# A layer's own products added by VectorE straight out of PSUM, and another order of work between the edge sort and layer 0

## Chip, cores and metric

The kernel runs on one core of a Trainium2 chip. The metric is the device time of one execution in microseconds (us). Times below come from three timed runs and from one profiled execution, whose trace gives the start and length of each instruction on the five engines: PE (matmul), DVE (VectorE), ACT (ScalarE), POOL (GpSimd) and SP (which only issues transfers here).

## The reference, cut to what matters

Two layers act on X, 6250 nodes with 256 features, over 100,000 weighted edges. In layer 0 the normalised rows go through two matrices: `x @ weight_l` gives the messages, which are gathered by source, weighted and summed by row, and `x @ weight_r` is the node's own product, added to the node itself with both biases:

```python
def _L0_gnn_ref(x, edge_row, edge_col, edge_val, weight_l, bias_l, weight_r, bias_r):
    h = x @ weight_l
    msgs = edge_val[:, None] * h[edge_col]
    agg = jax.ops.segment_sum(msgs, edge_row, num_segments=N)
    out = agg + bias_l
    out = out + x @ weight_r + bias_r
    return out
...
x = x + _L0_gnn_ref(_layernorm(x, axis=-1), src, dst, edge_weight, ...)
x = x + _L0_ffn_ref(_layernorm(x, axis=-1)[None], ...)[0]
x = x + _L1_gnn_ref(_layernorm(x, axis=-1), src, dst, edge_weight, ...)
x = x + _L1_ffn_ref(_layernorm(x, axis=-1)[None], ...)[0]
```

The feed-forward part of layer 0 has 8 experts of two hidden layers each, all of them computed and weighted by a softmax gate. Layer 1 sums messages by destination, and then computes 32 experts, of which each row keeps one.

## The kernel before, in words

X stays on the chip as 49 tiles of 128 rows. The work has three stages.

**The sort, 0 to about 391 us.** The edges have to be arranged by the tile of their row. They come in 25 groups (`for g in range(NG)`), and each group passes through four helpers. `count_group` makes one-hots of the tile of each edge (`hot` L454, `four`, `mine`) on VectorE and counts them by matmuls (L464 to L474); ACT evicts the counts as `start` (L472) and `total` (L476). `settle_group` keeps the running counts (`ZJ` L482, `wrap` L484, `base_of` L486, `full_of` L488). `place_group` works out each edge's place (`same` L497, `picked` L506, `pos` L516, `over` L519, `place_b` L521), makes the one-hot `to` (L523) from it, and multiplies the payload in five pieces into `loads` (four on VectorE, L527; one in 32 scaled activations on ACT, L502). PE's 32 `put` matmuls (L530) then throw the payload to its places; ACT evicts it as `there` (L533), and POOL adds it into Z (L535 to L539).

Layer 0's dense products ride along in the same loop, two tiles a group. `center0` takes bn_stats of X (L547) and centres X on ACT (`xn`, L556). `products0` transposes xn on PE, evicts the transpose on ACT (`nT`, L341), multiplies it with both matrices at once into one PSUM tile `ph` (L570; two halves of 256 columns, messages and own products), evicts all of `ph` on ACT, scaled by rstd (`hs`, L571), and POOL adds the second half and the bias to X (L572, L573). The first half is written to DRAM as h0 on SP's queue.

**Layer 0, to about 1830 us.** `edges0` reads a block's edges out of ZJ and Z into idx, w and dl (VectorE, L671 to L686). For each tile 18 indirect gathers are issued on POOL (L201); ACT and VectorE make m, the weighted row in two parts (L230, L231), VectorE makes one-hots s (L222), and PE sums into `acc` (L701), which VectorE adds to X (L704). These column steps form a stream (`aggregate0`), which a plan (`aheads`, `upto`) interleaves with the experts of the block before: `begin0` (norm, transposes, gates), `hidden0` (matmuls L748, eviction hT on ACT, L751), `outs0` (py L760, addition to X on VectorE, L762) and `end0` (h1, norm for layer 1). Blocks have 1, 1, 2, 3, then nine times 4, and 3 and 3 tiles. `missing` prepares what layer 1's early columns lack.

**Layer 1, to the end.** Gathers of h1 by sorted columns, then the 32 experts (`hidden1`, `outs1`, L984 to L1000), and the output.

The code gives the order in which a scheduler meets the instructions; the scheduler sets the order on each engine by its own priorities, and `tc.issue_after(ins)` pins an instruction behind another. Engines issue in order. Layer 0's weights (`w1`, `w2`, `wo`: 2 MB each) are loaded on ACT's queue when the sort's memory comes free, behind which `bo` and `gT` are cleared on VectorE (L641, L644).

Of the kernel before, what the change touches and what calls it, by code (L numbers as in the profile page):

```python
# [16 lines left out]
P = 128  # L17
N = 6250
D = 256
# [30 lines left out]
def gnn_ffn_kernel(ctx: ExitStack, tc: tile.TileContext, a, out):  # L50
# [59 lines left out]
    dl_c = const.tile([P, NCOL], F32, name="dl_c")  # L110
# [79 lines left out]
    bias0 = across("L0_gnn_bias_l", early)  # L190
    bias0r = across("L0_gnn_bias_r", early)
    nc.gpsimd.tensor_add(bias0, bias0, bias0r)
# [33 lines left out]
    def weighted(pool, h, idx, w, ahead, parts):  # L226

        g = gather(pool, h, idx, ahead)
        m = pool.tile([P, 2, D], F32R, tag="m", name="m", bufs=parts)
        nc.scalar.activation(m[:, 0, :], g, AF.Copy, scale=w)  # L230
        nc.vector.scalar_tensor_tensor(m[:, 1, :], g, w, m[:, 0, :], op0=OP.mult, op1=OP.subtract)  # L231
        return m

    halves = {}

# [101 lines left out]
    def transposed(psum, xn, to):  # L337
        tr = psum.tile([P, 2, P], F32, tag="tr", name="tr", bufs=1)
        for k in range(2):
            nc.tensor.transpose(tr[:, k, :], xn[:, k * P:(k + 1) * P], ident)  # L340
        nc.scalar.activation(to, tr, AF.Copy)  # L341

    def norm(psum, t, mean, rstd, to):

        xn = work.tile([P, D], F32, tag="xn", name="xn")
        nc.vector.tensor_scalar(xn, X[:, t, :], mean, rstd, op0=OP.subtract, op1=OP.mult)
        transposed(psum, xn, to)
# [99 lines left out]

    def count_group(g):
# [42 lines left out]
    def place_group(g, hot, start):  # L491
# [9 lines left out]
        for c in range(GC):  # L501
            nc.scalar.activation(loads[:, NPAY - 1, c // 4, :, c % 4], hot[:, c // 4, :, c % 4], AF.Copy,  # L502
                                 scale=last[:, g * GC + c:g * GC + c + 1])
# [9 lines left out]
        with nc.allow_low_precision(reason="counts below 256"):  # L513
            for h in range(2):
# [8 lines left out]
        nc.vector.tensor_tensor(to, place_b[:, :, None, :].to_broadcast([P, CB, P, 4]),  # L523
                                which_q[:, None, :, :].to_broadcast([P, CB, P, 4]), OP.is_equal)
# [10 lines left out]
        nc.gpsimd.tensor_add(there[:, 0], there[:, 0], there[:, 1])  # L535
        nc.gpsimd.tensor_scalar(some[:, 0], there[:, 0], 0.0, from_p[:, g:g + 1], op0=OP.is_gt, op1=OP.mult)
        nc.gpsimd.tensor_add(Z[:, 0, :, g], there[:, 0], some[:, 0])
        nc.gpsimd.tensor_add(some[:, 1], there[:, 2], there[:, 3])
        nc.gpsimd.tensor_add(Z[:, 1, :, g], some[:, 1], there[:, 4])  # L539

    def center0(tiles):

        n = len(tiles)
        mv = work.tile([P, NB, 2], F32, tag="mv", name="mv")
        for j, t in enumerate(tiles):
            st = work.tile([P, 6], F32, tag="st", name="st", bufs=4)
            nc.vector.bn_stats(st, X[:, t, :])  # L547
            nc.vector.bn_aggr(mv[:, j, :], st)
        std = work.tile([P, NB], F32, tag="std", name="std", bufs=3)
        nc.vector.tensor_scalar(std[:, :n], mv[:, :n, 1], LN_EPS, None, op0=OP.add)  # L550
        shift = work.tile([P, NB], F32, tag="shift", name="shift")
        nc.vector.tensor_scalar(shift[:, :n], mv[:, :n, 0], -1.0, None, op0=OP.mult)
        nc.scalar.activation(std[:, :n], std[:, :n], AF.Sqrt)
        xn = early.tile([P, 2, D], F32, tag="xn0", name="xn0", bufs=2)
        for j, t in enumerate(tiles):
            nc.scalar.activation(xn[:, j, :], X[:, t, :], AF.Identity, bias=shift[:, j:j + 1])  # L556
        return tiles, xn, std

    def products0(tiles, xn, std):
# [4 lines left out]
        hs = early.tile([P, 2, 2, D], F32, tag="hs", name="hs", bufs=2)  # L564
        for j, t in enumerate(tiles):
# [5 lines left out]
            nc.scalar.activation(hs[:, j], ph, AF.Copy, scale=rstd[:, j:j + 1])  # L571
            nc.gpsimd.tensor_add(X[:, t, :], X[:, t, :], hs[:, j, 1, :])  # L572
            nc.gpsimd.tensor_add(X[:, t, :], X[:, t, :], bias0)  # L573
        nc.sync.dma_start(h0[tiles[0] * P:(tiles[0] + n) * P, :].rearrange("(t p) d -> p t d", p=P), hs[:, :n, 0, :])
# [4 lines left out]
    centered = center0(pairs[0])  # L579
    settle_group(0, *counted[2:])  # L580
    for g in range(NG):
        now, tiles0 = counted, centered
        if g + 1 < NG:
            counted = count_group(g + 1)
        products0(*tiles0)
        place_group(g, *now[:2])
        if g + 1 < NG:
            centered = center0(pairs[g + 1])
            settle_group(g + 1, *counted[2:])
        if g == 1:  # L590
            check_edges()
            prep_ctx.close()
# [3 lines left out]
    nc.vector.tensor_reduce(most[:, 0:1], sizes.rearrange("p t g -> p (t g)"), AX.X, OP.max)  # L596
    tot = early.tile([P, NT], F32, name="tot")
    nc.vector.scalar_tensor_tensor(tot, full_of[0], float(P), base_of[0], op0=OP.mult, op1=OP.add)
    nc.vector.tensor_reduce(most[:, 1:2], tot, AX.X, OP.max)
    nc.vector.tensor_scalar(most[:, 0:1], most[:, 0:1], float(P), None, op0=OP.is_gt)  # L600
    nc.vector.tensor_scalar(most[:, 1:2], most[:, 1:2], float(P * EW), None, op0=OP.is_gt)
    nc.vector.tensor_max(bads[0], bads[0], most[:, 0:1])
    nc.vector.tensor_max(bads[0], bads[0], most[:, 1:2])
    nc.vector.tensor_copy(badis[0], bads[0])
    nc.vector.tensor_scalar(good, bads[0], 1.0, None, op0=OP.is_lt)
    nc.vector.tensor_max(bads[1], bads[1], bads[0])
    nc.vector.tensor_copy(badis[1], bads[1])
    nc.vector.tensor_scalar(good1, bads[1], 1.0, None, op0=OP.is_lt)
    nc.vector.tensor_scalar(off, bads[1], float(DST_PAD), None, op0=OP.mult)
    nc.vector.tensor_scalar(dl_c, dl_c, off, None, op0=OP.add)  # L610
# [24 lines left out]
    with tc.tile_pool(name="layer0", bufs=1) as wp, tc.tile_pool(name="outs0", bufs=1, side="right") as wo_pool, \  # L635
            tc.tile_pool(name="psum_y0", bufs=1, space=bass.MemoryType.PSUM) as psum_y:
        wr = wp.tile([P, 2, NX0], F32, name="wr")
        nc.scalar.dma_start(wr, a["L0_ffn_Wr"].rearrange("(k p) e -> p k e", p=P))

        bo = wp.tile([P, D], F32, name="bo")  # L640
        nc.vector.memset(bo, 0.0)  # L641
        nc.scalar.dma_start(bo[:NX0, :], a["L0_ffn_bo"])
        gT = wp.tile([P, NB * P], F32, name="gT")
        nc.vector.memset(gT, 0.0)  # L644
        bn = wp.tile([P, 2, 5, 2 * NX0], F32, name="bn")
        nc.scalar.dma_start(bn, a["bn"])
        wo = wo_pool.tile([P, NX0, 2, D], F32, name="wo")
        for w, name in ((w1, "L0_ffn_W1"), (w2, "L0_ffn_W2"), (wo, "L0_ffn_Wo")):
            nc.scalar.dma_start(w.rearrange("p e k h -> p (e k) h"), a[name].rearrange("e (k p) h -> p (e k) h", p=P))


        scale = wp.tile([P, 2, 2 * NX0], F32, name="scale")
        shift = wp.tile([P, 2, 2 * NX0], F32, name="shift")
        nc.vector.tensor_scalar(scale, bn[:, :, 4, :], BN_EPS, None, op0=OP.add)
        nc.scalar.activation(scale, scale, AF.Sqrt)
        nc.vector.reciprocal(scale, scale)
        nc.vector.tensor_mul(scale, scale, bn[:, :, 1, :])  # L657
        nc.vector.tensor_sub(shift, bn[:, :, 0, :], bn[:, :, 3, :])
        nc.vector.tensor_mul(shift, shift, scale)
        nc.vector.tensor_add(shift, shift, bn[:, :, 2, :])  # L660

        def edges0(tiles):
# [23 lines left out]
            nc.vector.tensor_copy(dl[:, :n], bothi[:, :n])  # L686
# [3 lines left out]
        edges = [edges0(blocks0[0]), edges0(blocks0[1])]  # L690

        def aggregate0():
            for b, tiles in enumerate(blocks0):
                idx, dl, w = edges[b]
                for i, t in enumerate(tiles):
                    acc = psum.tile([P, 2, D], F32, tag="agg", name="acc", bufs=2)
                    for j in range(EW):
# [3 lines left out]
                        nc.tensor.matmul(acc, s[:, j % SJ, :], m, start=(j == 0), stop=(j == EW - 1))  # L701
                        if j == EW - 1:
# [9 lines left out]
        def begin0(tiles):  # L712
# [5 lines left out]
            for j in range(n):  # L718
                for k in range(2):
                    nc.tensor.matmul(pl[:, j, :], nT[:, k, j * P:(j + 1) * P], wr[:, k, :],  # L720
                                     start=(k == 0), stop=(k == 1))
# [33 lines left out]
        def outs0(block, e, hT):  # L755
            tiles, _, gate = block
            for j, t in enumerate(tiles):
                py = psum_y.tile([P, D], F32, tag="y", name="py", bufs=2)
                for k in range(2):
                    nc.tensor.matmul(py, hT[:, k, j * P:(j + 1) * P], wo[:, e, k, :],  # L760
                                     start=(k == 0), stop=(k == 1))
                nc.vector.scalar_tensor_tensor(X[:, t, :], py, gate[:, j, e:e + 1], X[:, t, :],  # L762
                                               op0=OP.mult, op1=OP.add)
# [124 lines left out]
        plans[-1] = [cum[-1] + (NE - tail + CS // 2 + 3) * max(0, u + 1 - head) / (2 * NX0 - head) for u in range(2 * NX0)]  # L888
        sums.upto(cum[0])
        block = begin0(blocks0[0])  # L890
        first = hidden0(0, block, 0, block[1])
        for b in range(nblk):
            final = b + 1 == nblk
            for e in range(NX0):
                if e == 0 and b + 2 < nblk:
# [3 lines left out]
                if b == nblk - 3 and e == 3:  # L899
                    small1()  # L900
                    early_columns()
                if final and e == 5:
                    fill = missing()
                if final and e >= 5:
                    next(fill)
                sums.upto(plans[b][2 * e])
# [8 lines left out]
                sums.upto(plans[b][2 * e + 1])  # L915
# [194 lines left out]
```

## Time and profile before

| what | us |
|---|---|
| timed runs, median (lowest to highest) | 2901.26 (2896.87 to 2902.55) |
| profiled execution, its own time | 2895.13 |
| span of its trace | 2893.4 |
| mean granted TensorE clock (share of full speed) | 0.974 |
| busy: PE / DVE / ACT / POOL | 2677.7 / 2012.4 / 1626.1 / 1926.1 |
| from one `to` to the next in the sort (151.59 to 165.89) | 14.30 |
| last `to` of the sort starts | 379.28 |
| first gather of layer 0 | 397.79 |
| first `acc` matmul of layer 0 | 413.75 |

The profile cuts the span into 40 slices of 72 us, and gives each engine's busy tenths:

```profile
PE   5888848888999999999999998779999999999998
DVE  8999977778768767766566555666666666666630
PEclk9999978999999999999999999999999999999999
DMA  4000043333333333333332214333333333333310
```

A digit 9 is 90% or more; PEclk is the clock that TensorE was granted, in tenths. The first five slices are the sort, the sixth holds the crossing into layer 0, the 26th and its neighbours the crossing into layer 1. Timeline rows have the start, the length, the engine, the line, the operation with output and inputs, and in brackets the idle time before it with what ended it. Group rows have the count, then busy us and mean ns of one instruction, then idle before them and what released it.

### The profile page before, as it was taken

What the parts mean: (1) busy time and instruction counts of PE and PEld (TensorE: products, weight loads), DVE (VectorE), ACT (ScalarE), POOL (GpSimd) and SP (SyncE); (2) the same over time, 40 slices, a digit from 0 to 9 for tenths busy, and PEclk for the clock granted to TensorE, in tenths of its full rate; (3) what the DMA queues carried; (4) which work ended last, traced back from release to release, by engine and by line L of the source; (5) the groups of instructions that cost most, each with busy time, mean ns of one, the idle gap of its engine ahead of it and who ended that gap; (6) DMA issues with size and microseconds to landing.
All of it is one profiled execution on the core that took longest, in us unless ns stands there. A gap on an engine that the chain in (4) does not pass through costs nothing.

```text
span 2893.4 us, 37030 instructions
## 1 busy us (share of the span) xinstructions
PE 2677.7 (93%) x10336; PEld 1750.2 (60%) x10336; DVE 2012.4 (70%) x4917; ACT 1626.1 (56%) x3790; POOL 1926.1 (67%) x1932
## 2 busy tenths in 40 slices
PE   5888848888999999999999998779999999999998
PEld 2444427665566666666666665556666666666666
DVE  8999977778768767766566555666666666666630
ACT  6777737655555555555555545455555555555532
POOL 4666667777767676766675527677777777777720
PEclk9999978999999999999999999999999999999999
DMA  4000043333333333333332214333333333333310
GB/s 150 19 19 19 19 141 97 101 100 102 92 99 95 90 101 97 91 100 96 91 102 82 78 39 135 109 108 103 107 108 109 106 108 102 108 106 109 109 44 12
DMA packets 123140, 260.73 MB, mean 90 GB/s; under 512 B 32236, under 2 KB 68904, under 8 KB 122920
## 3 DMA queue, kind: packets, MB, share of 16 engines
q0 software_dynamic: 79872, 218.21, 26.2%
q1 hardware_dynamic: 31672, 32.42, 3.4%
q10 hardware_dynamic: 11376, 7.60, 0.8%
q8 instruction: 85, 1.39, 0.2%
q14 instruction: 135, 1.11, 0.1%
HBM read 238.87 MB, written 19.25 MB: 89 GB/s over the span
## 4 chain that ended last, share of the span: by engine, by line
PE 65%; DVE 17%; DMA 8%; issue 4%; ACT 4%; POOL 1%; ACTq 0%; POOLq 0%; DVEq 0%
PE ph L748 19%; PE py L760 10%; PE py L1000 9%; PE ph L984 9%; PE acc L701 6%; PE acc L277 4%; DMA g<-h,src_c 4%; DMA g<-h,idx 3%; DVE loads L527 3%; DVE to L523 2%; DVE m L231 2%; ACT m L230 2%; PE ph L987 1%; PE ph L214 1%; POOL g L201 1%
## 5 line engine op out<-in xcount | busy, mean ns | idle before, releaser
L201 POOL DMA_INDIRECT g<-h,idx x882 | 903.1, 1024 | 391.8 <-DVE m L231 175.2
L201 POOL DMA_INDIRECT g<-h,src_c x718 | 725.6, 1011 | 227.8 <-issue 104.2
L230 ACT ACTIVATE m<-g,w 128x256 fp32r<-128x256 f32 x882 | 394.7, 500 | 260.0 <-PE acc L701 136.0
L751 ACT ACTIVATE hT<-ph,shift,scale 128x512 f32<-128x512 f32 (+3 forms) x480 | 329.0, 696 | 314.6 <-PE ph L748 313.4
L230 ACT ACTIVATE m<-g,val_c 128x256 fp32r<-128x256 f32 x718 | 349.7, 503 | 273.6 <-PE acc L277 132.2
L231 DVE SCALAR_TENSOR_TENSOR m<-g,val_c,m 128x256 fp32r<-128x256 f32 x718 | 337.1, 483 | 211.2 <-ACT m L230 207.6
L231 DVE SCALAR_TENSOR_TENSOR m<-g,w,m 128x256 fp32r<-128x256 f32 x882 | 397.7, 476 | 42.5 <-ACT m L230 41.4
L748 PE MATMUL ph<-nT,w 128*128 128x512 f32 (+3 forms) x960 | 373.1, 524 | 25.0 <-ACT hT L751 24.8
L760 PE MATMUL py<-wo,hT 128*128 128x256 f32 x1568 | 382.1, 387 | 13.8 <-DVE X L762 10.5
L1000 PE MATMUL py<-w,hm 128*128 128x256 f32 x1568 | 386.7, 385 | 3.1 <-ACT hm L989 3.1
L701 PE MATMUL acc<-m,s 128*128 128x512 f32 x882 | 341.4, 490 | 38.0 <-DVE scale L657 24.7
L984 PE MATMUL ph<-nT,w 128*128 128x512 f32 (+2 forms) x832 | 374.8, 571 | 0.0
L748 PE MATMUL ph<-hT,w 128*128 128x512 f32 (+3 forms) x960 | 368.5, 518 | 0.5 <-ACT hT L751 0.5
L760 PEld LDWEIGHTS py<-wo,hT 128*128 128x128 f32 x1568 | 294.7, 193 | 80.8 <-DVE X L762 26.9
L277 PE MATMUL acc<-m,s 128*128 128x512 f32 x782 | 332.2, 499 | 1.7 <-DVE m L231 1.7
L1000 PEld LDWEIGHTS py<-w,hm 128*128 128x128 f32 x1568 | 292.1, 193 | 52.9 <-ACT hm L989 4.6
L222 DVE TENSOR_TENSOR s<-col,dl 128x384 fp32r<-128x384 f32 x294 | 161.4, 551 | 187.0 <-PE acc L701 184.8
L748 PEld LDWEIGHTS ph<-nT,w 128*128 128x128 f32 x960 | 175.2, 195 | 174.2 <-issue 118.1
L989 ACT ACTIVATE hm<-ph,b 128x512 f32<-128x512 f32 (+2 forms) x208 | 136.8, 659 | 200.0 <-PE ph L987 199.6
L748 PEld LDWEIGHTS ph<-hT,w 128*128 128x128 f32 x960 | 176.2, 193 | 118.9 <-issue 88.3
L701 PEld LDWEIGHTS acc<-m,s 128*128 128x128 f32 x882 | 169.7, 195 | 109.8 <-issue 48.9
L984 PEld LDWEIGHTS ph<-nT,w 128*128 128x128 f32 x832 | 157.2, 191 | 101.5 <-issue 81.1
(248 smaller groups left out, 3359.0 us busy)
## 6 DMA issues: line engine op xcount, KB each, us to landing
g<-h,idx POOLq DMA_INDIRECT x882, 2.8
g<-h,src_c POOLq DMA_INDIRECT x718, 2.8
h<-hs SPq DMA_DIRECT2D x25, 256.0 KB, 2.1
X<-in_x_dram SPq DMA_DIRECT2D x12, 512.0 KB, 8.9
out_dram<-o SPq DMA_DIRECT2D x11, 512.0 KB, 3.4
h<-hs SPq DMA_DIRECT2D x9, 512.0 KB, 3.0
w<-in_L_ffn_W_dram ACTq DMA_DIRECT2D x2, 2048.0 KB, 11.2
wo<-in_L_ffn_Wo_dram ACTq DMA_DIRECT2D x1, 2048.0 KB, 20.0
```

What stands on the lines that cost most here:

```text
L201: nc.gpsimd.indirect_dma_start(out=g, out_offset=None, in_=h, in_offset=bass.IndirectOffsetOnAxis(ap=idx, axis=0))
L222: nc.vector.tensor_tensor(s[:, :n], col[:, None, :].to_broadcast([P, n, P]), dl[:, j:j + n, None].to_broadcast([P, n, P]), OP.is_equal)
L230: nc.scalar.activation(m[:, 0, :], g, AF.Copy, scale=w)
L231: nc.vector.scalar_tensor_tensor(m[:, 1, :], g, w, m[:, 0, :], op0=OP.mult, op1=OP.subtract)
L277: nc.tensor.matmul(acc, s[:, (j - js.start) % SJ, :], m, start=opens, stop=done)
L701: nc.tensor.matmul(acc, s[:, j % SJ, :], m, start=(j == 0), stop=(j == EW - 1))
L748: nc.tensor.matmul(ph[:, :nw], (w1, w2)[layer][:, e, k, m * P:(m + 1) * P], src[:, k, :nw], start=(k == 0), stop=(k == 1))
L751: nc.scalar.activation(hT[:, m, :nw], ph[:, :nw], AF.Relu, bias=shift[:, layer, c:c + 1], scale=scale[:, layer, c:c + 1])
L760: nc.tensor.matmul(py, hT[:, k, j * P:(j + 1) * P], wo[:, e, k, :], start=(k == 0), stop=(k == 1))
L984: nc.tensor.matmul(ph[:, :nw], w1f[:, k, c * P:(c + 1) * P], nT[:, k, :nw], start=(k == 0), stop=False)
L989: nc.scalar.activation(hm[:, :nw], ph[:, :nw], AF.Relu, bias=b1[:, c:c + 1])
L1000: nc.tensor.matmul(py[:, j, :], now[:, cols], w2f[:, c, :], start=False, stop=(c == NC1 - 1), skip_group_check=True)
```

## The change

Layer 0's own products: ACT evicts only the messages' half of `ph`, 128x256 instead of 128x512. VectorE adds the other half to X in one scalar_tensor_tensor straight from PSUM (X = ph * rstd + X). POOL's two additions a tile are gone. The bias goes elsewhere: POOL splits the sum of both biases into three bf16 pieces at the start (rows 0, 32 and 64 of `bias0_b`), and each tile's `acc` in layer 0 gets one more bf16 matmul with `ones_b`. The second half of ACT's 32 scaled pieces is issued behind the pair's last eviction. The statistics of a pair are taken one group earlier (`stats0`).

The order between sort and layer 0: the last group's `to` is made in two halves, the checks stand behind it, and the last additions into Z go to VectorE. The first block's edges come first; the weights are loaded behind them on SP's queue, then the second block's edges. `wo`, whose memory is free early, is loaded in the sort: in the built order it stands on SP's queue right behind the second h0 write. The third block's edges come in the middle of the first block's columns. The columns that are issued beside the first two experts of the first block stand behind its norm, transposes and gates. `small1`, `early_columns` and `missing` stand behind the newest addition of `outs0`. `dl_c` becomes bf16. The blocks stay as they were.

The diff, cut to its core:

```diff
     def place_group(g, hot, start, evicted):
...
         for c in range(GC):
-            nc.scalar.activation(loads[:, NPAY - 1, c // 4, :, c % 4], hot[:, c // 4, :, c % 4], AF.Copy,
-                                 scale=last[:, g * GC + c:g * GC + c + 1])
+            with ExitStack() as behind:
+                for ins in evicted[-1:] if c >= GC // 2 else ():
+                    behind.enter_context(tc.issue_after(ins.ins))
+                nc.scalar.activation(loads[:, NPAY - 1, c // 4, :, c % 4], hot[:, c // 4, :, c % 4], AF.Copy,
+                                     scale=last[:, g * GC + c:g * GC + c + 1])
...
-        nc.vector.tensor_tensor(to, place_b[:, :, None, :].to_broadcast([P, CB, P, 4]),
-                                which_q[:, None, :, :].to_broadcast([P, CB, P, 4]), OP.is_equal)
+        final = g == NG - 1
+        step = CB // 2 if final else CB
+        for b in range(0, CB, step):
+            bs = slice(b, b + step)
+            placed = nc.vector.tensor_tensor(to[:, bs], place_b[:, bs, None, :].to_broadcast([P, step, P, 4]),
+                                             which_q[:, None, :, :].to_broadcast([P, step, P, 4]), OP.is_equal)
...
-            nc.scalar.activation(hs[:, j], ph, AF.Copy, scale=rstd[:, j:j + 1])
-            nc.gpsimd.tensor_add(X[:, t, :], X[:, t, :], hs[:, j, 1, :])
-            nc.gpsimd.tensor_add(X[:, t, :], X[:, t, :], bias0)
+            evicted.append(nc.scalar.activation(hs[:, j], ph[:, 0, :], AF.Copy, scale=rstd[:, j:j + 1]))
+            nc.vector.scalar_tensor_tensor(X[:, t, :], ph[:, 1, :], rstd[:, j:j + 1], X[:, t, :],
+                                           op0=OP.mult, op1=OP.add)
...
-        products0(*tiles0)
-        place_group(g, *now[:2])
+        evicted = products0(*tiles0)
+        placed, there, some = place_group(g, *now[:2], evicted)
         if g + 1 < NG:
-            centered = center0(pairs[g + 1])
+            end_group(g, there, some, nc.gpsimd)
+        if g + 1 < NG:
+            centered = center0(*measured)
+            if g + 2 < NG:
+                measured = stats0(pairs[g + 2])
             settle_group(g + 1, *counted[2:])
...
+    with tc.issue_after(told.ins):
+        end_group(NG - 1, there, some, nc.vector)
...
-        edges = [edges0(blocks0[0]), edges0(blocks0[1])]
+        told = []
+        edges = [edges0(blocks0[0])]
+        behind = ExitStack()
+        behind.enter_context(tc.issue_after(told[0].ins))
...
+        for w, name in ((w1, "L0_ffn_W1"), (w2, "L0_ffn_W2"), (wo, "L0_ffn_Wo")):
+            nc.sync.dma_start(w.rearrange("p e k h -> p (e k) h"), a[name].rearrange("e (k p) h -> p (e k) h", p=P))
...
+        edges.append(edges0(blocks0[1]))
+        behind.close()
...
                         nc.tensor.matmul(acc, s[:, j % SJ, :], m, start=(j == 0), stop=(j == EW - 1))
+                        if j == 0:
+                            nc.tensor.matmul(acc[:, 0, :], ones_b, bias0_b, start=False, stop=False,
+                                             skip_group_check=True)
...
+        sums.upto(cum[0] // 2)
+        with tc.issue_after(newest["rest"].ins):
+            edges.append(edges0(blocks0[2]))
         sums.upto(cum[0])
         block = begin0(blocks0[0])
+        normed = [newest[k] for k in ("xn", "nT", "gates")]
...
                 if b == nblk - 3 and e == 3:
-                    small1()
-                    early_columns()
+                    with tc.issue_after(newest["out"].ins):
+                        small1()
+                        early_columns()
```

In the changed code the eviction is line 604, the addition from PSUM line 605, `to` line 546 and the bias matmul line 752.

## Prediction

> **What bounds the kernel now.** I read the busy shares by stage first, because the change touches one stage and the crossing behind it. In these rows of the table of windows, the columns are window, its length, then PE, PEld, DVE, ACT and POOL busy (instructions), granted clock, DMA share, GB/s.
>
> ```profile
> 100.00:150.00 50.00, 43.60 (x201) 22.71 (x199) 50.00 (x109) 38.72 (x144) 29.91 (x35) 1.00 0.05 17
> 250.00:300.00 50.00, 43.65 (x188) 21.80 (x187) 50.00 (x109) 41.32 (x153) 34.42 (x38) 1.00 0.07 22
> 380.00:400.00 20.00, 7.40 (x32) 3.80 (x32) 12.60 (x47) 0.38 (x1) 6.34 (x9) 0.72 0.37 119
> 400.00:420.00 20.00, 6.24 (x13) 3.64 (x13) 19.45 (x54) 6.43 (x14) 15.92 (x14) 0.51 0.89 306
> ```
>
> In the sort VectorE is never idle; PE has 13% to spare. From 380 to 420 us PE is mostly idle: the crossing. So I went to VectorE's and POOL's timelines for one group of the sort. From one `to` (L523) to the next is 165.89 - 151.59 = 14.30 us; from the third group's `to` (80.1) to the last (379.28) 21 periods average 14.25.
>
> ```profile
> 151.59 2.27 DVE L523 TENSOR_TENSOR to<-place_b,which_q 128x4096 bf16<-128x4096 bf16 x1
> 153.94 0.76 DVE L482 SCALAR_TENSOR_TENSOR ZJ<-base_of,part,full_of 128x49 bf16<-128x49 bf16 x1
> 154.58 0.73 DVE L484 TENSOR_SCALAR wrap<-total 128x49 f32<-128x49 f32 x1
> 155.42 0.67 DVE L486 TENSOR_TENSOR base_of<-total,wrap 128x49 bf16<-128x49 f32 x1
> 156.97 0.88 DVE L497 TENSOR_TENSOR same<-tq 128x256 bf16<-128x256 bf16 x1
> ```
>
> ```profile
> 151.85 2.60 POOL L572 TENSOR_TENSOR X<-X,hs 128x256 f32<-128x256 f32 x1 [0.56 <-ACT hs L571]
> 154.53 0.74 POOL L573 TENSOR_TENSOR X<-X,L_gnn_bias_l_b 128x256 f32<-128x256 f32 x1
> 155.23 0.79 POOL L572 TENSOR_TENSOR X<-X,hs 128x256 f32<-128x256 f32 x1
> 156.09 1.47 POOL L573 TENSOR_TENSOR X<-X,L_gnn_bias_l_b 128x256 f32<-128x256 f32 x1
> ```
>
> The four VectorE operations lie beside POOL's four additions and take 0.76 + 0.73 + 0.67 + 0.88 = 3.04 us. Where POOL adds nothing, at 19 to 37 us, the same four took 0.41, 0.19, 0.20 and 0.40: 1.20. So the additions cost VectorE about 1.84 us a group, and its own work is 14.29 - 1.84 = 12.45.
>
> Then I read PE's and ACT's timelines of the same group, because the new operation waits for both.
>
> ```profile
> 153.92 7.38 PE L530 MATMUL put<-loads,to 128*128 128x245 bf16 x32
> 163.26 1.99 PE L570 MATMUL ph<-wlr,nT 128*128 128x512 f32 x4
> ```
>
> ```profile
> 162.84 0.37 ACT L341 ACTIVATE nT<-tr 128x256 f32<-128x256 f32 x1
> 165.33 0.69 ACT L571 ACTIVATE hs<-ph,rstd 128x512 f32<-128x512 f32 x1
> ```
>
> The reader is to see an order on PE: `put` (7.20 us until the count matmuls at 161.12), count, and only then the products `ph`. Nothing that leads to the next `to` depends on `ph` today.
>
> **The change in the sort.** Removed: POOL's four additions a pair (-1.84 us of VectorE's time). Added on VectorE: two scalar_tensor_tensor of 128x256 out of PSUM. The nearest row, which reads PSUM and X in the same form, is the layer's own addition:
>
> ```profile
> L762 DVE SCALAR_TENSOR_TENSOR X<-py,gate,X 128x256 f32<-128x256 f32 x392 | 186.7, 479 | 36.4 <-PE py L760 34.4
> L998 PE MATMUL py<-b,hotT 128*128 128x256 bf16 x49 | 13.4, 273 | 0.0
> ```
>
> Its 479 ns include overlap; start to start such additions follow each other at 0.39. VectorE's own work becomes 12.45 + 0.78 = 13.23 us. By work alone the sort would gain 1.06 us a group.
>
> But the additions are placed ahead of `to`. The built order of the changed kernel shows two kinds of group in turn. In kind A the first addition (L605) stands behind the loads and ahead of over, rstd, two bn_stats, place_b and `to`; the second stands behind `to`. In kind B both stand ahead of `to`, with two `loads` and pos between them. Each addition waits in that order for ACT's eviction of the other half of the same PSUM tile. `to` is what PE's next `put` waits for, and the `ph` that the addition reads stands on PE behind the previous `put`. So a loop closes that was open before. From the start of a `to`:
> - to the first `put` 153.92 - 151.59 = 2.33; 32 `put` 7.20; count 161.12 to 161.69, 0.57;
> - `ph` 163.26 to 165.08, 1.82; the two rest_tri matmuls ahead of the eviction's predecessor (`total`) 0.27; `total` and the eviction, now 128x256 like nT's 0.37, with handovers 0.6 to 0.7;
> - the addition 0.4 to 0.45;
> - over 0.18, rstd 0.10, bn_stats 0.34, place_b 0.16, bn_stats 0.34: 1.12.
>
> Sum for A: 2.33 + 7.20 + 0.57 + 1.82 + 0.27 + 0.65 + 0.4 + 1.1 = 14.3. For B comes what stands behind the waiting first addition: pos (0.30), loads (0.91), the addition to pos (0.11), loads (0.91), and the second addition 0.45: +2.6 to 2.7, 16.9. The second `ph` is then just out as well (its nT, 1.8 of products, nT and nine scaled pieces at 0.23, and an eviction end 6.1 us behind the `put`; VectorE comes there at 6.0). Mean (14.3 + 16.9) / 2 = 15.6 against 14.25: +1.35 a group; at the low end of the handovers A is 14.1 and B 16.7, +1.15. Over 21 periods: +24 to +28; I take +26. VectorE, busy 13.23 of 15.6, becomes idle ahead of L605; PE waits for `to` longer.
>
> ACT's shorter evictions (0.69 to 0.37, twice) and the second half of the scaled pieces behind the last eviction (16 x 0.23 = 3.7 us, chased by `put`'s second half, whose first half takes 3.6) are off this loop: 0. Early stats (bn_stats one group ahead): the same instructions, moved; in the sum above. The thirteen small POOL operations for the bias run in the first tens of us, where POOL idles: 0. dl_c in bf16 can only shorten L610 (0.63); the checks after the last `to` stay under `put`'s 7.2 us: 0, and some 2.9 us if that cover went.
>
> [...] The rows give 1.84 (the first addition began under `to` and waited itself: 2.60 us); I use 1.84. [...]
>
> **The crossing.** Before, the last `to` starts at 379.28, `put` ends at 389.0, ACT's `there` 389.1, POOL's Z to 390.99, then memsets and the edges of two blocks mixed on VectorE; idx at 396.81, first gather 397.79. After: `to` in halves lets `put` start 1.1 earlier; Z on VectorE takes about 5 x 0.12 = 0.6 instead of 1.44 (-0.85); with the first block's edges alone ahead, idx comes some 2.9 instead of 5.7 us behind Z (-2.8). Sum -4.7, taken as -4.5. The first matmul came at 413.75, 24.75 us late, because second edges and missing's operations stood ahead of m on VectorE; but the first tile's 18th gather was issued at 422.68 and its sum added at 428.72, so removing that queue gives no more than the gathers do (1.25 us each on POOL). The weights move to SP's queue: 4 MB instead of 6 MB fall on the gathers, at a DMA share of 0.89 and 306 GB/s before; the gathers' 3 to 5 us should shrink: 0 to -4, I take -2. Wo's 2 MB, 20.0 us to land, now go right behind the second h0 write. On SP's queue the next h0 writes (256 KB, 2.1 us) stand behind it; two hs buffers cover a period of about 15 us each. 0, at most +6, once.
>
> **Layer 0 and behind.** One bf16 matmul of 128x256 a tile: L998's row, 0.108 start to start, at worst 0.22 like `put`; 49 of them 5.3 to 11, most in the stage where PE decides, +4. Thirteen VectorE operations of missing move to the end of layer 0, where PE waits at times; small1's five DMAs pass SP's queue later, 0 to +3, taken 0. The first block's columns move behind its norm chain, where rstd waited 4.57 us at 437: 0 to -4, taken 0, since the following block hangs on the gathers. Blocks are as before.
>
> Sum against the profiled execution's 2895.13 (span 2893.4): +26 - 4.5 - 2 + 4 = +23.5, so 2918.6. The median of the three runs is 6.1 higher: 2901.26 + 23.5 = 2924.8.
>
> **Rivals.**
> - Faster: VectorE's work decides. If ACT and PE bring the eviction before VectorE has done its other work, L605 waits for nothing: -1.06 x 23 = -24, then -4.5 - 2 + 4: 2875. It decides as soon as both kinds' path is under 13.2 us, which needs `ph` ready 1.1 us (A) and 3.7 us (B) earlier than summed. For it: VectorE is 100% busy; against: PE's order, `put` ahead of `ph`. Chance 0.18.
> - Same: all groups run at A's 14.3, the second addition not holding anything: 0 - 4.5 - 2 + 4 = -2.5, 2899. [...] It would need the first half of B's additions earlier. Chance 0.07.
> - Slower still: h0 writes behind Wo (+6), the PE clock, 1.00 in the sort, falling in the new pauses as it did to 0.51 in the crossing (a tenth less on 13 us of PE a group is +1.3, 27 in all), or a crossing into layer 1 that missing disturbs: over 2940. Chance 0.05.
>
> **How the numbers follow.** The likeliest case has 0.70, with 2910 to 2940 as its own range: the handovers +-2, bias 0 to +6, DMA -2 to +2, crossing +-2, Wo up to +6, and A and B +-0.2 a group. No change means within 0.2% of 2901.26, 5.8 us, about what a measurement can tell. Slower by more 0.74 (a little of the likeliest case falls inside 0.2%), within 0.08, faster 0.18. To hold 8 in 10, the range goes from 2884, taking in the same case and the upper edge of the faster one, to 2940.
>
> **What would show it.** Right: L605 with long idle before it, released by ACT's hs; VectorE below 100 in the sort; `to` at alternating distances near 14.3 and 16.9; the last `to` near 405; first gather about 14 us behind it instead of 18.5; no POOL additions, and ZJ, wrap, base_of near 0.2 to 0.4. Wrong: `to` every 13.2 us with VectorE full. The forecast falls if the wait at L605 is short, since nothing else in the change costs more than 5 us.

## The result, and the profile after

The changed kernel takes 2930.64 us (median of four runs, 2930.02 to 2931.57); the kernel before took 2901.91 beside it (2896.87 to 2904.01). The ratio is 1.011, with a 95% interval of 1.0096 to 1.0124: 28 to 36 us slower. The forecast was 2924.8, slower with a chance of 0.74. The two profiled executions stand further apart than the medians, 2895.13 and 2930.02: a difference of 34.9 us, of which some 6 are the spread of the runs of before.

The windows of the sort and of the crossing, in the changed kernel (columns as before: window, length, PE, PEld, DVE, ACT, POOL, granted clock, DMA share, GB/s):

```profile
150.00:200.00 50.00, 38.27 (x173) 20.04 (x172) 41.49 (x104) 35.13 (x137) 6.21 (x18) 0.89 0.05 17
200.00:250.00 50.00, 41.07 (x185) 21.58 (x184) 43.53 (x108) 32.42 (x126) 7.11 (x18) 0.87 0.05 16
410.00:430.00 20.00, 7.38 (x32) 3.91 (x32) 11.83 (x40) 3.43 (x15) 0.81 (x1) 0.62 0.29 89
```

VectorE, which had been busy for at least 49.98 us of each 50 between 100 and 300 us, now idles 13 to 17% of the first two windows; POOL fell from 31 to 34 us in 50 to 6 or 7. PE lost busy time too. All three are idle at times, so what bounds the stage is no engine's work but a chain of waits. The table of waits between 100 and 400 us names it (engine and line, what ended the wait, us in total, times, the longest):

```profile
DVE X L605 <- ACT hs L604: 46.3, 28, 3.3
PEld L553 <- DVE to L546: 55.5, 20, 4.2
PE put L553 <- DVE to L546: 50.8, 20, 4.0
```

In before's sort nothing on VectorE waited for an eviction, and of PE's waits for `to` the same table has, for the weight load of `put`:

```profile
PEld L530 <- DVE to L523: 16.9, 20, 3.9
```

That is 0.7 us a group, and 3.9 once, ahead of the last group. The new addition waits for ACT's eviction, and behind it PE waits for `to`, 1.1 and 4.0 us in turn. VectorE's timeline shows the two kinds of group, A first (rows between them left out):

```profile
239.17 0.48 DVE L605 SCALAR_TENSOR_TENSOR X<-ph,rstd,X 128x256 f32<-128x256 f32 x1 [1.44 <-ACT hs L604]
239.57 0.17 DVE L537 TENSOR_SCALAR over<-pos 128x32 f32<-128x32 f32 x1
...
240.48 2.27 DVE L546 TENSOR_TENSOR to<-place_b,which_q 128x4096 bf16<-128x4096 bf16 x1
242.67 0.48 DVE L605 SCALAR_TENSOR_TENSOR X<-ph,rstd,X 128x256 f32<-128x256 f32 x1
...
253.46 0.48 DVE L605 SCALAR_TENSOR_TENSOR X<-ph,rstd,X 128x256 f32<-128x256 f32 x1 [3.32 <-ACT hs L604]
253.86 0.38 DVE L534 TENSOR_REDUCE pos<-picked 128x32 f32<-128x224 bf16 x1
254.16 0.97 DVE L550 TENSOR_TENSOR loads<-hot,pieces 128x1568 bf16<-128x1568 bf16 x1
...
255.14 0.97 DVE L550 TENSOR_TENSOR loads<-hot,pieces 128x1568 bf16<-128x1568 bf16 x1
256.28 0.48 DVE L605 SCALAR_TENSOR_TENSOR X<-ph,rstd,X 128x256 f32<-128x256 f32 x1 [0.17 <-ACT hs L604]
...
257.58 2.28 DVE L546 TENSOR_TENSOR to<-place_b,which_q 128x4096 bf16<-128x4096 bf16 x1
```

In A one addition with its wait lies ahead of `to`; in B the wait is 3.32 us, and pos, two loads and the second addition come behind it. `to` at 240.48 and 257.58 are 17.10 apart; the next comes at 271.88, 14.30 later. These two distances alternate to the end of the sort. The four operations that POOL's additions had stretched are short again: in the groups of 150 to 250 us ZJ has a mean of 0.42 us where it had 0.75, wrap 0.18 for 0.73, base_of 0.22 for 0.68, same 0.42 for 0.88, 1.80 us less in all.

Where the difference arises, read at the same points of both traces (us):

| point | before | after | later by |
|---|---|---|---|
| first `to` of the sort | 31.00 | 34.48 | 3.5 |
| fourth group's `to` | 80.09 | 83.49 | 3.4 |
| last group's `to` (first half) | 379.28 | 410.73 | 31.4 |
| first gather of layer 0 | 397.79 | 429.19 | 31.4 |
| first tile's sum added to X | 428.72 | 458.95 | 30.2 |
| first gate matmul | 441.37 | 466.74 | 25.4 |
| gates of the fifth block | 689.56 | 720.66 | 31.1 |
| gates of the sixth block | 798.98 | 826.35 | 27.4 |
| gates of the last block | 1713.06 | 1744.70 | 31.6 |
| first router matmul of layer 1 | 1838.26 | 1871.29 | 33.0 |
| span | 2893.4 | 2928.2 | 34.8 |

The crossing, on VectorE, from the last addition into Z to the first block's edges:

```profile
420.43 0.25 DVE L564 TENSOR_TENSOR Z<-there,some 128x49 f32<-128x49 f32 x1
424.81 0.40 DVE L689 TENSOR_TENSOR at<-ZJ,place 128x468 bf16<-128x468 bf16 x1 [4.13 <-DVEq L295]
```

Line 295 is no computation: it is the conditional branch to the pass that takes over when the edges don't fit. DVEq is VectorE's own sequencer. The view of this line (L294 before the change) has the branch and the sequencer's next entry in both traces: length in ns (minimum, median, maximum), then the start in us.

```profile
L294 DVEq COMPARE_BRANCH  x1: 72/72/72, 384.4 to 384.4; - x1
L294 DVEq EVENT_SEMAPHORE  x1: 21/21/21, 387.6 to 387.6; - x1
L295 DVEq COMPARE_BRANCH  x1: 72/72/72, 421.1 to 421.1; - x1
L295 DVEq EVENT_SEMAPHORE  x1: 21/21/21, 424.2 to 424.2; - x1
```

The branch itself takes 0.07 us, and some 3.1 us pass until the next entry, in both kernels. Before the change they lay under POOL's additions into Z, which ended at 390.99; now nothing covers them.

### The profile page after: what moved, and what is told of

Its sections match the earlier page's. It is cut to its first block, busy times and chain, and to the rows that moved or that the text cites. A ratio compares the mean times of both kernels' runs of the same rounds, so it can differ in the third digit from the quotient of the medians.

```text
span 2928.2 us, 36997 instructions
## 1 busy us (share of the span) xinstructions
PE 2679.0 (91%) x10385; PEld 1745.0 (60%) x10385; DVE 1995.2 (68%) x4972; ACT 1609.7 (55%) x3790; POOL 1767.7 (60%) x1843
## 4 chain that ended last, share of the span: by engine, by line
PE 62%; DMA 8%; DVE 6%; issue 5%; ACT 3%; POOL 2%; ACTq 0%; POOLq 0%; DVEq 0%
PE ph L800 19%; PE py L812 10%; PE py L1066 9%; PE ph L1050 8%; PE acc L750 6%; DMA g<-h,src_c 4%; PE acc L278 4%; DMA g<-h,idx 3%; DVE m L230 2%; POOL g L200 2%; ACT m L229 2%; PE ph L1053 1%; PE ph L213 1%; PE tr L341 1%; DMA g<-h,idx_e 1%
## 5 line engine op out<-in xcount | busy, mean ns | idle before, releaser
L800 PEld LDWEIGHTS ph<-nT,w 128*128 128x128 f32 x960 | 174.1, 194 | 175.8 <-issue 118.9
L553 PE MATMUL put<-loads,to 128*128 128x245 bf16 x800 | 184.6, 405 | 60.8 <-DVE to L546 60.8
```

The lines of the kernel that those rows point to most:

```text
L553: nc.tensor.matmul(put, to[:, c // 4, :, c % 4], loads[:, :, c // 4, :, c % 4], start=(c == 0), stop=(c == GC - 1))
L800: nc.tensor.matmul(ph[:, :nw], (w1, w2)[layer][:, e, k, m * P:(m + 1) * P], src[:, k, :nw], start=(k == 0), stop=(k == 1))
```

## The experiments

They ran later, on three chips on which layers 0 and 1 took longer (the kernel before 3227 to 3286 us; from 1000 to 1200 us PE was busy 184 to 193 us where it was 199.8); why, the record does not show. So times are compared only with the kernel before on the same chip, as ratios, and positions are read from the traces: the sort hardly differs there, and the last `to` of the changed kernel came at 412.4, within 2 us of the first comparison. A term of 5 us can't be told from the times of these chips.

**Both additions behind `to`.**

```diff
-            nc.vector.scalar_tensor_tensor(X[:, t, :], ph[:, 1, :], rstd[:, j:j + 1], X[:, t, :],
-                                           op0=OP.mult, op1=OP.add)
+            later.append((t, ph, rstd[:, j:j + 1]))
...
         placed, there, some = place_group(g, *now[:2], evicted)
+        with tc.issue_after(placed.ins):
+            for t, ph, r in later:
+                nc.vector.scalar_tensor_tensor(X[:, t, :], ph[:, 1, :], r, X[:, t, :], op0=OP.mult, op1=OP.add)
```

> The changed kernel, with both additions out of PSUM issued behind the group's one-hot `to` instead of ahead of it; nothing else differs. Theory (the loop: `to` stands behind an addition that waits for products which PE makes only behind the previous `put`): the loop opens, and a group then takes what VectorE has to do (13.2 us) or PE's own chain with its wait for the transpose (about 13.1 to 13.4): 21 periods of some 13.3 = 279 us where the changed kernel has 327, and 3.5 us less at the start. Time about 2880 us. Rival (the addition from PSUM is itself dear, or PE's chain needs 14.3 us whatever the additions do): periods of 14.3, time about 2900. Second rival (position does not matter): 2930.

Measured: 3189.95 against 3228.82 us, ratio 0.9877 (0.9829 to 0.9925). `to` comes every 13.2 to 13.3 us, the last at 353.98: 25.3 us ahead of the kernel before and 56.8 ahead of the changed one. Of VectorE, in this run:

```profile
211.20 2.33 DVE L546 TENSOR_TENSOR to<-place_b,which_q 128x4096 bf16<-128x4096 bf16 x1
213.45 0.86 DVE L625 SCALAR_TENSOR_TENSOR X<-ph,rstd,X 128x256 f32<-128x256 f32 x2
...
224.43 2.28 DVE L546 TENSOR_TENSOR to<-place_b,which_q 128x4096 bf16<-128x4096 bf16 x1
```

```profile
200.00:300.00 100.00, 93.38 (x417) 47.93 (x417) 100.00 (x255) 80.71 (x315) 39.28 (x43) 1.00 0.07 22
```

The same additions, two in 0.86 us without a wait; VectorE is full again, now with 13.2 to 13.3 us of work a group where 13.23 had been summed. The loop was the cause: neither the addition out of PSUM is dear, nor does PE's chain need 14.3.

**Only the second addition behind `to`.** The edit is the same, for `j == 1` alone.

> The changed kernel, with only the second addition of each pair issued behind `to`; the first stays ahead of it. Theory: every group becomes of kind A, 14.3 us apart, none at 17.1; about 27 us less, time about 2903, the sort as long as before the change. Rival (the 17.1 of every second group comes from something else than the second addition, as the loads or the scaled pieces on ACT): alternation stays, 2930.

Measured: ratio 1.0066 (1.0039 to 1.0093). The expectation was wrong: the groups still alternate, 14.3 and 16.46, and the last `to` comes at 404.56. Of the 2.8 us that kind B had more, 0.64 went. VectorE's timeline shows what remained:

```profile
234.08 0.48 DVE L609 SCALAR_TENSOR_TENSOR X<-ph,rstd,X 128x256 f32<-128x256 f32 x1 [3.35 <-ACT hs L605]
234.48 0.38 DVE L534 TENSOR_REDUCE pos<-picked 128x32 f32<-128x224 bf16 x1
234.77 0.96 DVE L550 TENSOR_TENSOR loads<-hot,pieces 128x1568 bf16<-128x1568 bf16 x1
...
235.75 0.97 DVE L550 TENSOR_TENSOR loads<-hot,pieces 128x1568 bf16<-128x1568 bf16 x1
236.64 0.17 DVE L537 TENSOR_SCALAR over<-pos 128x32 f32<-128x32 f32 x1
```

From the end of the waiting addition's slot (234.48) to over (236.64) stand 2.16 us of other work that needed no product at all and yet didn't start during the 3.35 us ahead of it: VectorE kept to the built order. The prediction's own sum for B had them; the expectation of this run had forgotten them.

**The loads ahead of the first addition.** All four loads are issued ahead of the first addition, which is pinned behind them, over behind it, and the second addition behind `to` (the core of the edit).

```diff
+            for k in range(NPAY - 1):
+                pk = pieces[:, k, cs].rearrange("p (b c) -> p b c", c=4)
+                loaded = nc.vector.tensor_tensor(loads[:, k], hot, pk[:, :, None, :].to_broadcast([P, CB, NT, 4]), OP.mult)
+            behind.enter_context(tc.issue_after(loaded.ins))
+            for t, ph, r in later:
+                firsts = nc.vector.scalar_tensor_tensor(X[:, t, :], ph[:, 1, :], r, X[:, t, :], op0=OP.mult, op1=OP.add)
...
+        over_behind.enter_context(tc.issue_after(firsts.ins))
...
+        placed, there, some, firsts = place_group(g, *now[:2], evicted, later[:1])
```

> The changed kernel, with the first addition of each pair behind all four loads of the group and still ahead of over and `to`, and the second behind `to`. Theory, mended after the run with only the second addition moved (where every second group still took 16.46): what makes kind B longer is that two loads and pos stand behind the waiting addition, 2.15 us, and the second addition adds 0.65. With nothing but over, two bn_stats and place_b behind the wait, every group takes 14.3, and the last `to` comes near 382, as early as before the change; time about the kernel before's plus 0 to 4. Rival (kind B has another cause, as PE's or ACT's turn of every second group): 14.3 and 16.5 go on in turn, time about before's plus 15.

Measured: ratio 0.9985 (0.9964 to 1.0006); `to` every 14.29 us, without alternation, the last at 380.61. So 14.3 is the length of the loop with the least behind the wait, 2.16 us are the loads and pos, 0.64 the second addition; together 17.1. The place of two additions in the order of one engine is worth some 57 us of the sort (56.8 between the traces of the changed kernel and of the first experiment), and all three cases are now apart.

**POOL adds again.** ACT evicts 128x512, POOL adds the second half; the bias stays a matmul.

```diff
-            evicted.append(nc.scalar.activation(hs[:, j], ph[:, 0, :], AF.Copy, scale=rstd[:, j:j + 1]))
-            nc.vector.scalar_tensor_tensor(X[:, t, :], ph[:, 1, :], rstd[:, j:j + 1], X[:, t, :],
-                                           op0=OP.mult, op1=OP.add)
+            evicted.append(nc.scalar.activation(hs[:, j], ph, AF.Copy, scale=rstd[:, j:j + 1]))
+            nc.gpsimd.tensor_add(X[:, t, :], X[:, t, :], hs[:, j, 1, :])
...
```

> The changed kernel with layer 0's own products evicted by ACT in one piece of 128x512 and added to X by POOL again, one addition a tile; the bias stays a matmul, and the order between sort and layer 0 stays. Theory: `to` waits for no products any more. VectorE's work is 12.45 us and about half of the 1.84 us that it lost beside POOL's four additions, some 13.3; the group takes 13.3 to 13.6, time about 2880 to 2890. Rival (POOL's two additions cost VectorE as much as the four did, or PE's chain binds at 14.3): 2900.

Measured: ratio 0.9871 (0.9803 to 0.994), `to` every 13.2 to 13.7 us, the last at 356.78, as expected. With the wait gone it hardly matters who adds: the two forms, 0.9877 and 0.9871, can't be told apart. Where do their 22 to 25 us against the kernel before come from? VectorE is full in all three (99.8 us and more of 100), so its own row of work tells. From start to start, its small operations on counts and statistics (ZJ, wrap, full_of, base_of, same, std and shift) take 3.07 us a group before, 2.14 with POOL's one addition a tile, and 1.25 with none, and the two additions on VectorE cost 0.79. So POOL's bias additions alone had cost 0.93 us a group, and with all of POOL's additions gone the balance is 1.03; some 20 us over the sort. The rest, 3 us of it in the last group, no run takes apart.

**No branch.** The conditional pass between sort and layer 0 is left out.

```diff
-        aggregate_any(psum, h0, False)
```

> The changed kernel without the pass between sort and layer 0 that takes over when the edges do not fit the sort's places, and so without the conditional branch that all engines take there; for these inputs the pass is never entered. Theory: VectorE's 4.13 us between the last addition into Z and the first edges are the branch, which lay under POOL's additions before the change: they go, the first gather comes some 14.3 us behind the last `to` instead of 18.5, and the time is about 2926.5. Rival (the 4 us are a wait for something else, as a transfer or memory that comes free): they stay, 2930.

Measured: VectorE goes on 0.25 us after its last addition into Z instead of 4.13, and the first gather comes 425.82 - 411.24 = 14.6 us behind the last `to` instead of 18.5:

```profile
420.94 0.25 DVE L564 TENSOR_TENSOR Z<-there,some 128x49 f32<-128x49 f32 x1
421.44 0.40 DVE L687 TENSOR_TENSOR at<-ZJ,place 128x468 bf16<-128x468 bf16 x1 [0.25 <-DVE Z L564]
```

So the wait belongs to the branch and its pass. The ratio, 1.0069 (1.005 to 1.0088), agrees with 4 us less but doesn't show it.

**Z on POOL again, additions behind `to`.**

```diff
-    with tc.issue_after(told.ins):
-        end_group(NG - 1, there, some, nc.vector)
+    end_group(NG - 1, there, some, nc.gpsimd)
```

> Both additions behind `to` (as in the run that took 0.988 of the kernel before), and the last group's additions into Z on POOL again instead of VectorE. Theory: VectorE passes the branch (4.1 us) while POOL adds, so that the first edges follow POOL's last addition at once; POOL is 0.9 us slower; the first gather comes 15 to 15.7 us behind the last `to` instead of 18.4, the time is 3 us less than with VectorE's additions. Rival (POOL's own branch delays the gathers by as much): 18.4 stays, or more.

Measured: ratio 0.9904 (0.9874 to 0.9934). The first gather comes 368.24 - 353.18 = 15.1 us behind the last `to`, where with VectorE's additions it had been 372.38 - 353.98 = 18.4. VectorE's next operation starts as soon as POOL has ended:

```profile
363.87 0.40 DVE L691 TENSOR_TENSOR at<-ZJ,place 128x468 bf16<-128x468 bf16 x1 [4.71 <-POOL Z L564]
```

POOL takes 1.43 us for these five operations (362.40 to 363.83), VectorE 0.78 where they were its own (363.16 to 363.94, with both additions behind `to`). So the slower engine is the better one for them, since VectorE passes its branch meanwhile (at 359.4 in this trace). The times can't show 3 us. The same kernel once more, beside the changed one:

> Both additions behind `to` and the last additions into Z on POOL, as in the run that gave 0.990 of the kernel before on a chip whose layers took 380 us longer; now beside the changed kernel. Theory: the last `to` at 353 and the first gather at 368, 61 us ahead of the changed kernel; the bias costs 5 us; some 59 us less than the changed kernel and 28 less than the kernel before, if nothing behind gives it back. Rival (the layers give part of it back): 20 to 45 us less than the changed kernel.

Measured: 3190.28 us, ratio 0.9896 (0.9862 to 0.9929), 63 us less than the changed kernel on that chip and 36 less than the kernel before, a little more than expected. It beats both kernels.

**The changed kernel again.**

> The changed kernel as it is, beside the others on the same chip. Both theories: 1.010 to 1.012 of the kernel before where layers 0 and 1 run as in the first comparison; its difference to the kernel before is some 30 us, and the sort's last `to` comes 31.4 us later, wherever it runs.

Measured: 3252.9 us, 26 us above the kernel before, ratio 1.006 (1.0028 to 1.0092), below the expected 1.010 to 1.012; the interval ends just below where that of the first comparison (1.0096) begins. The last `to` came at 412.38, 33.1 us later than in before's trace.

**No bias matmul**, twice; the biases are then missing from X.

```diff
-                        if j == 0:
-                            nc.tensor.matmul(acc[:, 0, :], ones_b, bias0_b, start=False, stop=False,
-                                             skip_group_check=True)
```

> The changed kernel without the bias matmul of layer 0 (the biases are left out of X, so part of the computation is missing). Theory: the matmul costs PE 0.1 us a tile where PE decides; a block of four tiles takes 105.2 instead of 105.6 us, 4 to 5 us in all, nothing before the fifth block. Rival (it hides in PE's waits): blocks of 105.6 stay, 0. Other rival (a bf16 matmul among f32 ones costs a weight load of its own, as 0.22 of `put`): 11 us less.

> The changed kernel without the bias matmul (the biases are left out of X), once more beside the changed kernel. Theory: 0.11 to 0.12 us a tile where PE decides, 4 to 5 us in all. Rival: it hides, 0. On a chip where the blocks take 116 us, gathers decide and nothing is to be seen.

Measured: ratios 1.0072 (1.0053 to 1.009) and 1.008 (1.0048 to 1.0111), against 1.006 with the matmul. Inconclusive: on these chips blocks of four tiles take 111 to 122 us, and 0.15% isn't to be seen. What the first comparison shows stands in the next section.

**wo late.** A memset of two columns of wo behind the first edges holds its load in the crossing.

```diff
         wo = wo_pool.tile([P, NX0, 2, D], F32, name="wo")
+        nc.vector.memset(wo[:, 0, 0, 0:2], 0.0)
```

> The changed kernel with the 2 MB of wo loaded behind the other two weights in the crossing (a small memset of wo behind the first edges holds it), instead of in the sort. Theory: with 6 MB on the way the first gathers land later; from the first gather to the first gate matmul it takes some 43 us as before the change instead of 37.5; 3 to 6 us more in that place, and 0 to 5 in the time. Rival (the 6 us came from the order of VectorE's work, not from the transfer): 37.5 stays.

Measured: from the first gather (429.48) to the first gate matmul (467.00) it takes 37.5 us as in the changed kernel. The transfer did move: the DMA share from 440 to 460 us is 0.64, where the changed kernel has 0.37. The theory fell: the 6 us are not the transfer's.

**The first block's columns free again.**

```diff
-                for ins in normed if b == 0 and e < 2 else ():
+                for ins in ():
```

> The changed kernel without the pins that put the first block's columns behind its norm, transposes and gates. Theory: the pins gave what the trace shows behind the first tile's sum (from the sum's addition to the gate matmul 7.8 us instead of 12.65 before the change), so that without them it takes some 12 to 13 again; but the following blocks hang on the gathers, which go on at the same pace, so that from the fifth block on and in the time nothing changes: the changed kernel's time within 2 us. Rival (the 5 us come from the other order of VectorE's work, or they are carried to the end): 7.8 stays; or the time is 5 us more.

Measured: from the first sum's addition (461.70) to the gate matmul (475.12) 13.4 us, where the changed kernel took 7.8 on the same chip (462.29 to 470.13); 4.83 of it are VectorE's wait for ACT's square root, as the 4.57 of before: ACT comes to the square root only behind scaled rows m, each of which waits for its gather (0.7 to 1.1 us each in this trace). So the pins gave it. At the fifth block both are level (774.6 and 777.0): given back. The expectation of an unchanged time did not come true: the median is 25 us above the changed kernel's (ratio to the kernel before 1.0157, 1.0122 to 1.0192, clear of 1.0028 to 1.0092), while the profiled execution is 18 us shorter (spans 3256.0 and 3273.9). The traces don't show where the 25 us arise, so what these pins are worth in the end stays open.

## Why the prediction was right, and where its terms were off

**The sort, +26 forecast, +31.4 measured.** The mechanism was the forecast one: a loop over PE's `put`, the products, ACT's eviction and the addition ahead of `to`. Kind A was summed to 14.3 and took 14.30; B to 16.9 and took 17.10. That A fits so closely is partly luck: from the end of `ph` to the addition it took 1.07 us (269.50 to 270.57) where 0.92 had been summed, and from there to `to` 1.31 instead of 1.5. Over 21 periods the sort grew by (410.73 - 83.49) - (379.28 - 80.09) = 28.0, the upper end of the 24 to 28 that had been worked out. (80.1, in the prediction the third group's `to`, is the fourth's; its 21 periods are right.) The other 3.4 us arise ahead of the first `to`, which the sum had left out: two waits at L605, 0.69 and 0.33 us, and both additions stand ahead of it, and so do three bn_stats more than before, since the statistics are taken a group earlier. The prediction had put these at nothing; that they are the rest is likely, since with both additions behind `to` the first one still came at 32.69. Wo's load in the sort, feared at up to 6 us, cost nothing to be seen: it was issued at 60.4, and the delay is 3.5 us at the first `to` and 3.4 at the fourth.

The faster rival (VectorE's work decides, 13.23 us a group, about -24 in the sort) named the right price for a kernel that isn't this one: with the additions behind `to` the sort was 25.3 us shorter (20.0 in twenty periods of a full group, the rest in the first groups and the last, so the match with 24 is partly chance). It failed on the condition that it stated, `ph` 1.1 and 3.7 us earlier; the waits at L605 were 1.44 and 3.32.

**POOL's additions.** The 1.84 us beside them were right: 1.80 went. On the PSUM tile that ACT and VectorE share from now on, ACT's half runs from 252.96 to 253.43, and VectorE's starts at 253.46, as in the built order. No run lets the two overlap, so what the order costs is not shown.

**The crossing, -4.5 forecast, 0 measured (18.51 and 18.46 us from `to` to the first gather, where about 14 had been forecast).** The failed step is "with the first block's edges alone ahead, idx comes some 2.9 instead of 5.7 us behind Z". Both shortcuts came: Z was complete 11.7 us after `to` before (379.28 to 390.99) and 9.9 after; and in the run without the branch the first gather follows Z in 4.6 us (421.19 to 425.82) instead of 6.8. But the branch came into the open. Before, VectorE went through it from 384.4 to 387.6, while POOL still added; now VectorE itself adds last, and comes to the branch behind that, at 421.1. The prediction had no term for it: timelines and groups of before book VectorE's wait to POOL's Z, and only the view of line 294 has the branch. What fills the 3.1 us behind the branch's 0.07 is not shown. PE has the like (3.5 us, from 416.0 to 419.5), while POOL and SP go on within 0.2. In the code the pass that is skipped has 981 operations for VectorE and 882 matmuls for PE, but 18 gathers for POOL and two transfers for SP: the two engines that skip much have the long gap. No run varies the length of the pass, so whether it is the cause is not shown.

**The gathers, -2 forecast.** From the first gather to the first tile's sum 30.9 us became 29.8: -1.2, and the run with wo late shows that the moved weights are not what shortened the way to the gates. **The norm chain, 0 forecast (0 to -4):** from that sum to the gates 12.65 us became 7.8, -4.9, by the pins. "The following block hangs on the gathers" was right: by the fifth block the kernel was 31.1 us behind again; what the pins do to the whole time is open, as the run without them says.

**The bias, +4.** Its row is as forecast, near L998's:

```profile
L752 PE MATMUL acc<-bias_b,ones_b 128*128 128x256 bf16 x49 | 13.9, 284 | 0.0
```

In the four blocks between the gates at 798.98 and 1219.30 (before) a block took 105.08; after (826.35 to 1248.55) 105.55. That is 0.47 for four tiles, 0.12 a tile, and the delay grows from 27.4 to 31.6 between the sixth and the last block: +4.2. This is read from two traces; no experiment confirms it alone.

**What stays open.** Between the gates of the fifth and the sixth block the changed kernel won back 3.7 us, and from the last block's gates to the end it lost 3.2; the cause of either is open, and the four runs of before alone lie up to 7.1 us apart. In sum the forecast's +23.5 became +28.7 in the medians and +34.9 in the profiled executions: the start of the sort (3.4) and the branch (4.1) are the two terms that were missing, and the periods, at 28 for 26, the one that was sized too low.

## What to carry to other kernels

Ahead of moving work to an engine, follow in the built order what its new wait stands in front of: here two additions of 0.4 us, placed ahead of the operation that opens PE's next piece, closed a loop and cost some 57 us against the same additions behind it. An engine's sum of work bounds a stage only as long as nothing on it waits for what it has itself to release: VectorE's 13.23 us a group became 13.2 to 13.3 with the additions behind `to`, but 14.3 and 17.1 in turn with them ahead. And where a step between stages is moved to the faster engine, look for what the other was hiding, here 4.1 us of a branch: timelines and groups show it only once something waits for it, the view of its line at any time.

## What the runs showed of the hardware

- Passing over a conditional pass that is not entered cost VectorE 4.1 us between two operations (3.9 to 4.1 in four other runs), and 0.25 with the pass left out. In the changed kernel's trace the load of the condition takes 0.54 us (from 420.4), the branch 0.07 (at 421.1); the sequencer's next entry comes at 424.2, the next operation at 424.81. In these five runs the cost shows as idle time released by the engine's own sequencer (DVEq).
- In windows of 50 us between 100 and 350 us the granted clock was 0.87 to 0.93 in the changed sort, where PE paused for 4 us in every second group, and 1.00 before. Within them the clock is 0.50 for stretches of 3.4 or 6.8 us and 1.00 between, and from 100 to 400 us only `put` matmuls start in such a stretch. They follow each other at 225 ns at either clock (255 and 337 of them), so no matmul became longer: `put` took 405 ns in the mean against 406, and `ph` 616 against 618 (150 to 250 us). The risk of 27 us named for this did not come.
- ACT's eviction `hs` of 128x512 took 688 ns in the mean, of 128x256 466: half the size, 0.68 of the time. The forecast's 0.37, from nT's row, was 0.1 short.
